# Three of five large projections by Strassen's algorithm, in a graph-attention and feed-forward kernel on one core

## The chip, the cores and the metric

The kernel runs on one core of one Trainium2 chip. A core has a matrix engine (TensorE, in the profile PE for its matmuls and PEld for its weight loads), VectorE (DVE), ScalarE (ACT), GpSimd (POOL) and SyncE (SP, here used to issue DMAs). The metric is the device time of one execution in microseconds, and of several runs the median. A profile is one execution, recorded by the hardware profiler.

## The reference, cut to what matters

Everything is fp32. `x` is 384 x 1024, all weights of the attention part are 1024 x 1024, the feed-forward part has a hidden width of 512.

```python
n = layernorm(x)
q, k, v = n @ wq.T + bq, n @ wk.T + bk, n @ wv.T + bv
q2, k2, v2 = q @ wiq.T + biq, k @ wik.T + bik, v @ wiv.T + biv      # then 16 heads of 64
scores = q2 @ k2.T / 8 + mask          # per head; mask from 12288 edges, -inf where there is none
x = x + (softmax(scores) @ v2) @ wo.T + bo
n = layernorm(x)
h = silu(n @ w1.T * s1) * (n @ w2.T * s2)
h = gelu(h @ h1.T * t1)
h = gelu(h @ h2.T * t2)
return x + h @ w3.T * s3
```

The mask is a 384 x 384 table: each edge (source, target, type) writes one value, the last edge of a cell wins, and the diagonal has a default.

## The kernel before, in words

Activations are held transposed (features on the 128 partitions, in 8 groups of 128, and the 384 rows in the free dimension), so that weights are TensorE's stationary operand and a projection needs no transposition. `matmul_T` (L139) makes one output group of 128 features: 8 matmuls of 128 x 128 weights with 384 columns, accumulated in one PSUM bank. `project` (L382) runs over two halves of the weights, each with four output groups; ScalarE writes each result to SBUF with the bias added (L391). The chain is qT from xT, q2T from qT, vT from xT, then v2 (rows on partitions, `matmul_R` at L148, 512 columns, evicted by VectorE at L404), then kT from xT. k2T is made in steps of one matmul (`project_k2`, L440): 24 steps ahead, the rest between the attention units.

Weights arrive in halves of 2 MB (`load_w`, L81) in a ring of four buffers; `prefetch` issues the next half on SP's queue. It waits until the half that it replaces has been read.

Beside the projections runs the making of the mask. Per chunk of 8 columns of 128 edges, `keys` (L325) reads the keys of the chunk back from memory, `targets` (L334) finds on VectorE the edges that a later edge overwrites, and `scatter` (L354) issues 8 indirect DMAs from POOL, each waiting for the one two before it. There are 12 chunks. In the program of VectorE all chunks stand ahead of the projections' own work, in SP's program the reads of the keys stand between the first weight loads. After the last scatter POOL reads the table back into `nmask` (L378), which every score reduction (L475) needs, and then adds the output bias to `xs` (L409).

The order on SP, ACT, DVE and PE is the order of the code (a manual schedule); each of these engines runs its instructions strictly one after the other, and waits on semaphores that the framework places. [...] two for the projections (`ps_mm`), the others for pools that open and close with the stages.

In the feed-forward part (`rest`, L616) ScalarE computes Silu at L687, and Gelu at L703 from h1 and h2. Before Gelu its table has to be loaded, which happens ahead of the first Gelu. `inspect` (L178) reads the feed-forward weights in pieces and sums the low halves of their words on ScalarE (L186), to choose between two ways of computing; the one used here has two fp32r products per weight.

Of the kernel before, what the change touches and what calls it, by code (L numbers as in the profile page):

```python
# [8 lines left out]
FP = mybir.dt.float32  # L9
FR = mybir.dt.float32r  # L10
BF = mybir.dt.bfloat16
# [4 lines left out]
ALU = mybir.AluOpType  # L16
# [11 lines left out]
NCOL = E // P  # L28
DEEP = 2
# [12 lines left out]
def gnn_ffn_kernel(ctx: ExitStack, tc: tile.TileContext, x, edges, etw, vecs, rows,  # L42
# [28 lines left out]
    row = const.tile([P, 3, F], FP, name="row")  # L71
# [5 lines left out]
    def load_rows():  # L77
        nc.sync.dma_start(row, bass.AP(tensor=rows.tensor, offset=rows.offset,
                                       ap=[[0, P], [F, 3], [1, F]]))
# [29 lines left out]
    biqs = const.tile([P, KF], FP, name="biqs")  # L109
# [68 lines left out]
    def inspect(raws):  # L178
        for raw in raws:
            at = lows.shape[1] - len(pieces)  # L180
            w, i = pieces.pop(0)
            nc.sync.dma_start(raw, bass.AP(tensor=w.tensor, offset=w.offset + i * P * F,
                                           ap=[[F, P], [1, F]]))
            low = raw.bitcast(U16).rearrange("p (f two) -> p f two", two=2)[:, :, 0]
            junk = stage.tile([P, F], BF, tag="junk", name="junk", bufs=1)
            nc.scalar.activation(junk, low, AF.Copy, accum_out=lows[:, at:at + 1])  # L186
# [3 lines left out]
    k2T = act.tile([P, KF, N], FP, name="k2T")  # L190
    v2 = act.tile([P, NT, F], FP, name="v2")
    xT = act.tile([P, KF, N], FP, tag="xT", name="xT")

    with tc.tile_pool(name="edge", bufs=1) as ep, tc.tile_pool(name="krow", bufs=2) as krp, \
# [20 lines left out]
        later = ep.tile([P, DEEP * P], FP, name="later")  # L215
# [149 lines left out]
        nc.vector.tensor_scalar(biqs, vec[:, BIQ:BIQ + KF], -0.125, None, op0=ALU.mult)  # L365
        for c0 in range(0, NCOL, CHUNK):
            kr = keys(c0)
            if c0 == 0:
                nc.sync.dma_start(cells, bare)
                prefetch()  # L370
            targets(c0, kr)
            if c0 == 0:
                values()
            scatter(c0)
            if c0 in (2 * CHUNK, 5 * CHUNK):
                prefetch()
        load_rows()
        read = nc.gpsimd.dma_start(nmask, cells).ins  # L378
        for i in sent[-DEEP:]:
            after(read, i)  # L380

        def project(src, name, bias, dst=None, scale=1.0):  # L382

            if dst is None:
                dst = act.tile([P, KF, N], FP, tag="t", name=name, bufs=2)
            for half in range(2):
                (w,) = queue.pop(0)
                for i in range(4):
                    o = 4 * half + i
                    ps = matmul_T(w, src, i)  # L390
                    nc.scalar.activation(dst[:, o, :], ps, AF.Identity, bias=bias[:, o:o + 1],  # L391
                                         scale=scale)
                prefetch()
            return dst

        qT = project(xT, "qT", vec[:, BQ:])
        project(qT, "q2T", biqs, dst=q2T, scale=-0.125)
        vT = project(xT, "vT", vec[:, BV:])
        for half in range(2):
            (w,) = queue.pop(0)  # L400
            c = slice(half * FH, (half + 1) * FH)
            for t in range(NT):
                ps = matmul_R(w, vT, t)
                nc.vector.tensor_add(v2[:, t, c], ps, row[:, 0, c])  # L404
            prefetch()

        for t in range(NT):
            tc.keep_in_program_order(
                nc.gpsimd.tensor_add(xs[:, t, :], xs[:, t, :], row[:, 1, :]))  # L409
        kT = project(xT, "kT", vec[:, BK:])  # L410
# [4 lines left out]
    aT = act.tile([P, KF, N], FP, tag="xT", name="aT")  # L415
    ps_ff = ctx.enter_context(tc.tile_pool(name="ps_ff", bufs=4, space=bass.MemoryType.PSUM))
# [17 lines left out]
    with tc.tile_pool(name="attn", bufs=1) as ap, \  # L434
# [5 lines left out]
        def project_k2():  # L440

            for o in range(KF):
                ps = ps_mm.tile([P, 512], FP, tag="mm", name="ps")
                for k in range(KF):
                    nc.tensor.matmul(ps[:, :N], lhsT=wik[o // 4][:, k, o % 4 * P:(o % 4 + 1) * P],  # L445
                                     rhs=kT[:, k, :], start=(k == 0), stop=(k == KF - 1))
                    if k == KF - 1:
                        nc.scalar.activation(k2T[:, o, :], ps[:, :N], AF.Identity,  # L448
                                             bias=vec[:, BIK + o:BIK + o + 1])
                        if o % 4 == 3:  # L450
                            early.append(load_w(*ffn[o // 4], rounded=True))
                    yield
# [163 lines left out]
    def rest(fast):  # L616
# [59 lines left out]
        for o in range(KH):  # L676
# [14 lines left out]
            if fast:  # L691
                nc.scalar.copy(g[0][:, o, :], full)
                remainder(g[1][:, o, :], full, g[0][:, o, :])

# [17 lines left out]
        for some in (ends[:3], *([e] for e in ends[3:])):  # L712
# [3 lines left out]
            for (t, a, b), (p, _) in zip(some, ps):  # L716
                nc.vector.tensor_mul(y[:, t, a:b], p, row[:, 2, a:b])  # L717
                nc.vector.tensor_add(y[:, t, a:b], y[:, t, a:b], xs[:, t, a:b])  # L718
                nc.sync.dma_start(out[t * P:(t + 1) * P, a:b], y[:, t, a:b])
# [39 lines left out]
```

## Time and profile before

| | us |
|---|---|
| median of 3 runs (414.23 to 414.82) | 414.78 |
| the profiled execution | 414.55 |
| its span in the trace | 412.8 |
| PE busy in the span | 402.2 |
| DVE busy | 151.4 |
| ACT busy | 114.7 |
| POOL busy | 109.9 |

A line of the list of groups reads: line of the kernel, engine, operation, output <- inputs (names without numbers), shapes, count, then busy time and the mean duration in ns of one, then the idle time of the engine just before them with what ended it. Durations of one engine can overlap: instructions are pipelined, so a mean duration is longer than the distance from one start to the next. In the chain of work that ended last, columns are the start, the length, and the engine and line that the chain went through. A line of the timeline has start, length, engine, line, operation, and in brackets the idle time before and what ended it. In the view of stretches each engine has its busy time and its number of instructions; then come the granted TensorE clock, the share of DMA, and GB/s. The 1.8 us between span and execution time are outside the trace.

### The profile page before, as it was taken

Reading aid. Unit: us, or ns where it says so; the run is one execution under the profiler, and the core shown is the slowest. Engines: PE = TensorE matmul, PEld = TensorE weight load, DVE = VectorE, ACT = ScalarE, POOL = GpSimd, SP = SyncE. Lnnn points to the kernel's source line nnn. Section 1 sums busy time; section 2 is a strip of 40 time slices with the busy share of each in tenths; the row PEclk is TensorE's granted clock in tenths of the full one; section 3 lists DMA queues with packets and bytes.
Section 4 is the critical chain, followed back from the end, with each engine's and each line's share of the span. In section 5 each row is a group of like instructions: output and inputs, shape, how many; then the busy total and the mean of one; then the engine's idle time right before and its main releaser. Section 6 shows DMA issues by size and latency. Waiting matters only on the chain.

```text
span 412.8 us, 4295 instructions
## 1 busy us (share of the span) xinstructions
PE 402.2 (97%) x1549; PEld 244.0 (59%) x1549; DVE 151.4 (37%) x525; ACT 114.7 (28%) x249; POOL 109.9 (27%) x117
## 2 busy tenths in 40 slices
PE   7899999999999999999999999999999999999993
PEld 7555555555555444455555555555554444699883
DVE  5637968600000001000000167866763045322455
ACT  4511111111111000001112156757672177132320
POOL 3023344332656465756474010000000000200000
PEclk9999999999999999999999999999999999999998
DMA  7699655997050505050517216111088040560004
GB/s 273 215 333 290 220 192 164 370 388 251 3 204 0 203 2 204 0 204 2 204 21 261 82 39 215 52 51 52 1 265 287 9 153 0 171 239 0 0 3 155
DMA packets 29208, 59.65 MB, mean 145 GB/s; under 512 B 4384, under 2 KB 7296, under 8 KB 29056
## 3 DMA queue, kind: packets, MB, share of 16 engines
q1 hardware_dynamic: 22016, 49.89, 35.1%
q0 software_dynamic: 6880, 9.03, 7.6%
q10 hardware_dynamic: 288, 0.41, 0.3%
q8 instruction: 14, 0.23, 0.2%
q14 instruction: 10, 0.08, 0.1%
HBM read 57.06 MB, written 2.26 MB: 144 GB/s over the span
## 4 chain that ended last, share of the span: by engine, by line
PE 90%; DVE 4%; ACT 3%; DMA 1%; issue 1%; SPq 0%; ACTq 0%
PE ps L144 40%; PE ps L153 10%; PE ps L445 10%; PE ps L424 8%; PE ps L625 6%; PE av L502 4%; PE sc L461 4%; PE pp L493 4%; PE ps L637 3%; DMA xs<-in_x 1%; DVE y L718 1%; DVE y L717 1%; DVE st L114 1%; ACT junk L186 1%; ACT e L477 1%
## 5 line engine op out<-in xcount | busy, mean ns | idle before, releaser
L356 POOL DMA_INDIRECT tab<-val,cell x96 | 94.4, 983 | 113.7 <-DMA tab<-val,cell 64.3
L475 DVE CUSTOM_DVE_ANT_0 e<-sc,nmask 128x384 f32<-128x384 f32 x48 | 23.9, 553 | 60.0 <-PE sc L461 59.9
L340 DVE SCALAR_TENSOR_TENSOR jk<-kr,key,later 128x256 bf16<-128x256 f32 x96 | 39.8, 479 | 13.9 <-DMA kr<-keyd 13.9
L445 PE MATMUL ps<-kT,wik 128*128 128x384 f32 x128 | 43.4, 487 | 0.0
L424 PE MATMUL ps<-wo,aT 128*128 128x512 f32 x96 | 42.5, 593 | 0.0
L144 PE MATMUL ps<-xT,wq 128*128 128x384 f32 x128 | 41.5, 487 | 0.3 <-ACT xT L260 0.3
L144 PE MATMUL ps<-qT,wiq 128*128 128x384 f32 x128 | 41.4, 486 | 0.0
L144 PE MATMUL ps<-xT,wv 128*128 128x384 f32 x128 | 41.4, 486 | 0.0
L144 PE MATMUL ps<-xT,wk 128*128 128x384 f32 x128 | 41.4, 486 | 0.0
L153 PE MATMUL ps<-wiv,vT 128*128 128x512 f32 x96 | 41.4, 592 | 0.0
L404 DVE TENSOR_TENSOR v<-ps,row 128x512 f32<-128x512 f32 x6 | 4.1, 691 | 95.9 <-PE ps L153 95.9
L144 PEld LDWEIGHTS ps<-xT,wk 128*128 128x128 f32 x128 | 24.3, 190 | 17.2 <-issue 0.5
L144 PEld LDWEIGHTS ps<-xT,wq 128*128 128x128 f32 x128 | 24.2, 190 | 17.2 <-ACT xT L260 0.5
L144 PEld LDWEIGHTS ps<-qT,wiq 128*128 128x128 f32 x128 | 24.3, 190 | 17.0
L144 PEld LDWEIGHTS ps<-xT,wv 128*128 128x128 f32 x128 | 24.3, 190 | 17.0
L477 ACT ACTIVATE e<-e,lo 128x384 f32<-128x384 f32 x48 | 28.9, 604 | 12.0 <-DVE lo L475 11.4
L445 PEld LDWEIGHTS ps<-kT,wik 128*128 128x128 f32 x128 | 23.5, 190 | 14.6 <-ACT k2T L448 0.5
L153 PEld LDWEIGHTS ps<-wiv,vT 128*128 128x128 f32 x96 | 18.2, 190 | 22.7 <-issue 22.5
L424 PEld LDWEIGHTS ps<-wo,aT 128*128 128x128 f32 x96 | 17.7, 190 | 20.2 <-issue 20.2
L391 ACT ACTIVATE kT<-ps,vec 128x384 f32<-128x384 f32 x8 | 4.6, 581 | 77.8 <-PE ps L144 77.8
L625 PE MATMUL ps<-x,w 128*128 128x384 f32 (+2 forms) x176 | 25.8, 307 | 0.0
L625 PEld LDWEIGHTS ps<-x,w 128*128 128x128 f32 x176 | 25.1, 190 | 0.5 <-issue 0.5
(112 smaller groups left out, 367.6 us busy)
## 6 DMA issues: line engine op xcount, KB each, us to landing
kr<-keyd SPq DMA_DIRECT2D x11, 576.0 KB, 5.6
raw<-in_w SPq DMA_DIRECT2D x12, 512.0 KB, 4.8
w<-in_w POOLq DMA_DIRECT2D x3, 2048.0 KB, 11.0
wiq<-in_wiq SPq DMA_DIRECT2D x2, 2048.0 KB, 14.0
wv<-in_wv SPq DMA_DIRECT2D x2, 2048.0 KB, 15.4
wiv<-in_wiv SPq DMA_DIRECT2D x2, 2048.0 KB, 14.6
wk<-in_wk SPq DMA_DIRECT2D x2, 2048.0 KB, 8.3
wik<-in_wik SPq DMA_DIRECT2D x2, 2048.0 KB, 7.6
```

The costliest lines, as they stand in the source:

```text
L144: nc.tensor.matmul(ps[:, :N], lhsT=w[:, k, o * P:(o + 1) * P], rhs=src[:, k, :], start=(k == 0), stop=(k == nk - 1))
L153: nc.tensor.matmul(ps[:, :w.shape[2]], lhsT=src[:, k, t * P:(t + 1) * P], rhs=w[:, k, :], start=(k == 0), stop=(k == nk - 1))
L340: nc.vector.scalar_tensor_tensor(jk[:, :w], krf[:, j * P:j * P + w], key[:, c:c + 1], later[:, :w], op0=ALU.is_equal, op1=ALU.mult, accum_ ...
L356: i = nc.gpsimd.indirect_dma_start(out=tab, in_=val[:, c:c + 1], in_offset=None, out_offset=bass.IndirectOffsetOnAxis(ap=cell[:, c:c + 1], ...
L424: nc.tensor.matmul(ps, lhsT=aT[:, k, t * P:(t + 1) * P], rhs=wos[half][:, k, :], start=k == 0, stop=k == KF - 1)
L445: nc.tensor.matmul(ps[:, :N], lhsT=wik[o // 4][:, k, o % 4 * P:(o % 4 + 1) * P], rhs=kT[:, k, :], start=(k == 0), stop=(k == KF - 1))
L461: nc.tensor.matmul(sc[:, :N], lhsT=q2T[r, pair, t * P:(t + 1) * P], rhs=k2T[r, pair, :], start=True, stop=True)
L475: nc.vector.tensor_tensor_reduce(e, sc[:, :N], nmask[:, t, :], 1.0, 3e38, op0=ALU.add, op1=ALU.min, accum_out=lo)
L477: nc.scalar.activation(e, e, AF.Exp, bias=lo, scale=-1.0, accum_out=dens[u][:, j:j + 1])
L493: nc.tensor.transpose(pt[:, m, :], e[:, m * P:(m + 1) * P], ident)
L502: nc.tensor.matmul(av[j * D:(j + 1) * D, :N], lhsT=v2[:, m, h * D:(h + 1) * D], rhs=pTs[pair % 2][:, j * NT + m, :], start=(m == 0), stop= ...
L625: nc.tensor.matmul(ps[:, rows], lhsT=w[:, k, o * P:(o + 1) * P], rhs=x[:, k, rows], start=n == 0, stop=n == len(todo) - 1)
```

## The change

The projections q2, v and k are computed by Winograd's form of Strassen's algorithm, one level deep. Features in (two halves of 4 groups), features out (two weight halves) and rows (two halves of 192) are halved. Seven products of 4 x 4 matmuls with 192 columns take the place of eight such (64 matmuls of 384 columns before). The weight sums are made in place in the weight buffers and in one extra buffer `t3`; the sums of the source are four blocks `sums`, made once from xT (used by v and k) and once from qT. Results are put together by VectorE from PSUM and from what is already in the output; ScalarE copies only the first product. q and v2 keep their form; v2 and k2T take their inputs in the order 4 to 7, 0 to 3.

Other edits: the chunks of the mask are no longer all ahead, but one by one between the steps of the projections, on VectorE and SP; weight loads are issued in pairs after q2, v and k; `ps_st` has 6 banks; the factor -0.125 moves from q2T to k2T; the three constant rows take two places, and the third row is loaded later; `later` lies in `jp`; the sums of the low halves are written in place instead of into `junk`; k2T and v2 share memory with the sums; and an activation of one column with Gelu is put behind the Silu stage.

```diff
-            junk = stage.tile([P, F], BF, tag="junk", name="junk", bufs=1)
-            nc.scalar.activation(junk, low, AF.Copy, accum_out=lows[:, at:at + 1])
+            nc.scalar.activation(low, low, AF.Copy, accum_out=lows[:, at:at + 1])
...
-        for c0 in range(0, NCOL, CHUNK):
-            kr = keys(c0)
-            if c0 == 0:
-                nc.sync.dma_start(cells, bare)
-                prefetch()
-            targets(c0, kr)
-            if c0 == 0:
-                values()
-            scatter(c0)
-            if c0 in (2 * CHUNK, 5 * CHUNK):
-                prefetch()
-        load_rows()
+        krs = [keys(0)]
+        nc.sync.dma_start(cells, bare)
+        def chunk():
+            c0 = len(sent)
+            if c0 + CHUNK < NCOL:
+                krs.append(keys(c0 + CHUNK))
+            targets(c0, krs.pop(0))
+            if c0 == 0:
+                values()
+            scatter(c0)
...
+        def row_sums(src, tag):
+            sums = act.tile([P, 4, HK, HN], FP, tag=tag, name="sums")
+            s1, s2, s3, s4 = (sums[:, i] for i in range(4))
+            (a11, a12), (a21, a22) = ([src[:, k:k + HK, r:r + HN] for k in (0, HK)]
+                                      for r in (0, HN))
+            minus(s3, a11, a21)
+            nc.vector.tensor_add(s1, a21, a22)
+            minus(s2, s1, a11)
+            minus(s4, a12, s2)
+            return s1, s2, s3, s4
+        def third(at=0):
+            b11, b12, b21, b22 = blocks(at)
+            t3 = tp.tile([P, HK, FH], FP, tag="t3", name="t3")
+            minus(t3, b22, b12)
+            return t3
+        def first():
+            b11, b12, b21, b22 = blocks()
+            minus(b12, b12, b11)
+        def product(w, x):
+            ps = [ps_st.tile([P, 2, 256], FP, tag="st", name="ps") for _ in range(2)]
+            for o in range(4):
+                for k in range(HK):
+                    nc.tensor.matmul(ps[o // 2][:, o % 2, :HN], lhsT=w[:, k, o * P:(o + 1) * P],
+                                     rhs=x[:, k, :], start=(o % 2, k) == (0, 0),
+                                     stop=(o % 2, k) == (1, HK - 1))
+            return [p[:, :, :HN] for p in ps]
...
+            def plus(to, ps, more):
+                for p in range(2):
+                    o = slice(2 * p, 2 * p + 2)
+                    nc.vector.tensor_add(to[:, o, :], ps[p], more[:, o, :])
+            def finish(to, ps, more, column):
+                for o in range(4):
+                    nc.vector.scalar_tensor_tensor(
+                        to[:, o, :], ps[o // 2][:, o % 2, :], bias[:, column + o:column + o + 1],
+                        more[:, o, :], op0=ALU.add, op1=ALU.add)
+            m1 = product(b11, a11)
+            for p in range(2):
+                nc.scalar.copy(c11[:, 2 * p:2 * p + 2, :], m1[p])
+            beside[0]()
+            m7 = product(t3, s3)
+            nc.vector.tensor_add(b11, b11, t3)
+            beside[1]()
+            m6 = product(b11, s2)
+            plus(c12, m6, c11)
+            plus(c21, m7, c12)
+            m2 = product(b21, a12)
+            beside[2]()
+            finish(c11, m2, c11, 0)
+            minus(b21, b21, b11)
+            m5 = product(b12, s1)
+            plus(c12, m5, c12)
+            finish(c22, m5, c21, HK)
+            beside[3]()
+            finish(c12, product(b22, s4), c12, HK)
+            finish(c21, product(b21, a22), c21, 0)
+            for _ in range(2):
+                queue.pop(0)
+                prefetch()
...
-        qT = project(xT, "qT", vec[:, BQ:])
-        project(qT, "q2T", biqs, dst=q2T, scale=-0.125)
-        vT = project(xT, "vT", vec[:, BV:])
+            prefetch()
+            chunk()
+            prefetch()
+            chunk()
+            prefetch()
+            sums_x = row_sums(xT, "k2T")
+            chunk()
+            load_rows(0, 0, 2)
+            qT = project(xT, "qT", vec[:, BQ:])
+            t3 = third()
+            first()
+            chunk()
+            sums_q = row_sums(qT, "v2")
+            t3s = []
+            project_fast(qT, sums_q, t3, q2T, vec[:, BIQ:],
+                         [nothing, chunk, chunk, lambda: t3s.append(third(2))])
+            vT = act.tile([P, KF, N], FP, tag="t", name="vT", bufs=2)
+            project_fast(xT, sums_x, t3s[0], vT, vec[:, BV:], [first, chunk, chunk, chunk])
+            v2 = act.tile([P, NT, F], FP, tag="v2", name="v2")
             for half in range(2):
...
+                prefetch()
+                for _ in range(2 - half):
+                    chunk()
+                if half == 0:
+                    t3 = third(1)
...
-        kT = project(xT, "kT", vec[:, BK:])
+            kT = act.tile([P, KF, N], FP, tag="t", name="kT", bufs=2)
+            project_fast(xT, sums_x, t3, kT, vec[:, BK:], [first, nothing, nothing, nothing])
...
+        loaded = small.tile([P, 1], FP, name="loaded")
+        nc.scalar.activation(loaded, eps, AF.Gelu)
```

`blocks` names the four blocks of two weight halves: left half's upper and lower inputs are b11 and b21, the right half's are b12 and b22. Products are numbered here in the order in which they run: m1, m7, m6, m2, m5, and the two last ones. `chunk` in the list `beside` puts one chunk of the mask's work at that point.

## The prediction

> **What bounds the kernel now.** First the page's busy times and the chain that ended last:
>
> ```profile
> span 412.8 us, 4295 instructions
> PE 402.2 (97%) x1549; PEld 244.0 (59%) x1549; DVE 151.4 (37%) x525; ACT 114.7 (28%) x249; POOL 109.9 (27%) x117
> PE 90%; DVE 4%; ACT 3%; DMA 1%; issue 1%; SPq 0%; ACTq 0%
> ...
> PE ps L144 40%; PE ps L153 10%; PE ps L445 10%; PE ps L424 8%; PE ps L625 6%; PE av L502 4%; PE sc L461 4%; PE pp L493 4%; PE ps L637 3%; DMA xs<-in_x 1%; DVE y L718 1%; DVE y L717 1%; DVE st L114 1%; ACT junk L186 1%; ACT e L477 1%
> ```
>
> TensorE is the chain: L144, the four projections q, q2, v and k, is 40% of the span alone. The change touches three of them. Next the chain in order of time, for lengths without overlap, and the groups kept apart by shape:
>
> ```profile
> 12.96 124.08 PE ps L144 x384
> 137.04 41.20 PE ps L153 x96
> 178.24 41.28 PE ps L144 x128
> ```
>
> ```profile
> L144 PE MATMUL ps<-qT,wiq 128*128 128x384 f32 x128 | 41.4, 486 | 0.0
> L144 PEld LDWEIGHTS ps<-qT,wiq 128*128 128x128 f32 x128 | 24.3, 190 | 17.0
> L718 DVE TENSOR_TENSOR y<-y,xs 128x512 f32<-128x512 f32 x5 | 3.5, 693 | 0.2
> L718 DVE TENSOR_TENSOR y<-y,xs 128x256 f32<-128x256 f32 x2 | 0.8, 425 | 0.1
> L531 DVE COPY pTa<-pp 128x384 f32<-128x384 f32 x12 | 6.7, 557 | 9.9 <-PE pp L493 9.9
> L689 DVE SCALAR_TENSOR_TENSOR gf<-ps,vec,sl 128x384 f32<-128x384 f32 x4 | 2.5, 618 | 14.5 <-PE ps L625 14.5
> ```
>
> A projection of 64 fp32 matmuls leaves 128 records. Records of 384 columns follow each other at 41.28/128 = 322.5 ns, those of 512 columns at 41.20/96 = 429.2 ns: 0.833 ns a column and 2.5 ns for the record. (The 486 of the page is a duration with drain; it overlaps.) PE has no idle time here, and its weight loads are idle 17 of 41 us: they hide. Other engines in those 206 us, by the view of stretches (columns: PE, PEld, DVE, ACT, POOL busy):
>
> ```profile
> 13.00:54.00 41.00, 41.00 (x128) 24.17 (x129) 26.68 (x125) 7.35 (x12) 10.53 (x10) 1.00 0.83 270
> 54.00:95.00 41.00, 41.00 (x129) 24.17 (x128) 21.74 (x108) 4.66 (x8) 15.99 (x16) 1.00 0.77 269
> 95.00:137.00 42.00, 42.00 (x132) 24.77 (x131) 0.00 (x0) 4.66 (x8) 24.36 (x26) 1.00 0.30 101
> ```
>
> DVE is empty from 95 us on; that is the room the change uses.
>
> [...] 32 of the 128x256 records of L625 take 3.83 us of the chain, 120 ns each, each with its load. [...] In this trace a scatter instruction takes 1.0 to 1.2 us beside DVE work and 0.97 later, so little. [...]
>
> **The change part by part.**
>
> *PE.* Each of q2, v, k becomes seven products of 4 x 4 matmuls of 192 columns: 112 matmuls, 224 records instead of 128. At 192 x 0.833 + 2.5 = 162.5 ns these take 36.4 us. The old ones took 41.36 (124.08/3), 41.36 and 41.28. Saved: 4.96 + 4.96 + 4.88 = 14.8 us, if the records stay at that pitch. No 192-column fp32 record is in the trace. Below: 160 ns is pure streaming, 35.8 us. Above: the only records [...] are the fp32r ones of 384 columns at L625; 59 of them touch 10 us of trace, some 172 ns each, giving 38.5 us and a saving of only 8.5 us in all. I take 162.5: the 2.5 ns is the same at 384 and 512 columns of fp32[...].
>
> *DVE.* Per projection four sums of 2048 elements (t3, b12, b11, b21) at 2.29 us = 9.2; six adds from PSUM of 384 elements at 0.56 (the L531 duration) = 3.3; twelve finishes of 192, estimated as L689's 618 less 192 elements at 1.05 = 0.42 us, = 5.0: 17.5 us. Row sums of xT and qT: eight of 768 at 0.96 = 7.7. Together 60 us, on top of 52.6 busy in that stretch, in some 191 us. So DVE is not the bound by volume; order decides. With E the start of a projection, products of 5.2 us, and an edge chunk of 3.7 us (18.18 to 21.92 us in the timeline):
> Product 3 needs b11+t3, which waits for product 1 to have read b11: E+5.4+2.3 = 7.7, against 10.4. In k DVE comes from the last chunk and `first()`, and is done near E+9.0: 1.4 to spare, the tightest.
> Product 5 needs the banks of product 2, freed by the four adds after product 3: E+15.8+2.2 = 18, against 20.8.
> Product 7 needs b21-b11: after a chunk and finishes, E+25.6, against 31.2.
> The v2 matmuls need vT's finish of product 6, behind v's third chunk: E+33.9, against 36.4; they begin with the late inputs' half that is ready first, and the last finish hides behind four matmuls.
> All on time, so the sums cost nothing while DVE keeps this order; a DVE that is 3 us late in a projection starts to stall PE.
>
> *SP.* The key reads are now issued between weight loads. In v, the keys of its second chunk stand behind wiv0 and wiv1, which wait for q2's last product. The DMA row reaches 370 and 388 GB/s in 72 to 93 us; 4.2 MB and 0.6 MB of keys at that pace with 2 us of latency land near E+15; the chunk comes at E+18. In q2 the keys behind wv1 land near 65 us, the chunk can begin as late as 68. Nothing on the path.
>
> *POOL.* The scatters and the mask:
>
> ```profile
> 211.20 0.97 POOL L356 DMA_INDIRECT tab<-val,cell  x1 [0.30 <-issue]
> 213.96 0.80 POOL L378 DMA_DIRECT2D nmask<-tab  x1 [1.79 <-DMA tab<-val,cell]
> ```
>
> The read takes 4.3 us to land, at 218.3; the first score row needs it at 235.88, and after the change at 221.1. A scatter costs 1.28 us undisturbed (most of 103 to 117 us), nearer 2.5 under loads (16 in 54 to 95). After: some 15 by 66 us as before, 19 more by 91 (no weight load then, chunks 4 to 6 ready), and 62 at 1.6 (the 26 in 42 of the stretches): last at about 191, mask near 198. The last chunk is ready near 173, not binding.
>
> *ACT.* The Gelu load:
>
> ```profile
> 386.95 1.28 ACT L703 ACT_TABLE_LOAD   x1 [2.27 <-PE ps L637]
> 388.25 1.05 ACT L703 ACTIVATE gf<-ps,vec 128x384 f32<-128x384 f32 x2
> ```
>
> ```profile
> 383.24 5.71 PE L637 MATMUL ps<-g,h 128*128 128x384 f32 x32
> 389.28 0.45 PE L637 MATMUL ps<-g,h 128*128 128x384 f32 x1 [0.32 <-DVE g L705]
> 389.87 5.67 PE L637 MATMUL ps<-g,h 128*128 128x384 f32 x31
> ```
>
> The dummy goes behind the last copy of the gate (ends 384.7), so the load ends at 386.0 in ACT's idle time. ACT gains 1.28, but PE works on the fourth output until about 388.8 (388.95 less drain), then loses 0.5 ahead of 389.28 and 0.4 ahead of 389.87. That 0.9 is the gain; then PE is what is late. The in-place copy of the raw pieces (1.06 us each) keeps its elements: taken as nothing, bounded by 0.5 us either way, as ACT waits anyhow in those stages. Bias and scale moved to k2T: same instruction count.
>
> Sum: 414.55 of the profiled run - 14.8 - 0.9 = 398.9; the median (414.78) stands 0.2 above that run: 399.1 us. Attention moves up whole.
>
> **The rivals.**
> (1) PE stalls at seams: DVE late by waiting for keys or by slower sums. For: DVE is strict in order, and a chunk that waits for keys holds finishes that free banks. Against: the margins above. Each stall is 1 to 3 us in one or two projections: 400.5 to 405.
> (2) Records of 192 columns keep 172 ns: 414.8 - 8.5 - 0.9 = 405.4, with small waits 405 to 408. For: the fp32r records. Against: fp32 records show no such gap.
> (3) The mask comes late. If POOL contends with the 2.3 us sums and chunks wait, the scatters end after 215 and the first scores wait at L475 while PE goes on only with the k2T steps left. It costs from a mask at 221.1 on, and decides for slower at 221.1 + 15.7 = 236.8, when the last scatter is at 231: a mean of (231-24.65)/96 = 2.15 us a scatter, against 1.95 before (a few us more if k2T steps fill in). At the 2.5 of the loaded stretch throughout, the last is at 265 and the mask lands near 271, 50 us late, of which k2T steps in PE's order fill perhaps 5: 399 + 45 = 444, an estimate. Against: the loads end sooner, and POOL has 30 us of slack by my count.
> (4) The dummy is useless, if Gelu's load stays where it was: 400.0. The program of the change has a load ahead of the dummy and none ahead of Gelu, so unlikely; it is inside the first range.
>
> **How the numbers follow.** Forecast (398 to 400.5) 0.62; stalls (400.5 to 405) 0.18; record gap (405 to 408) 0.12; better than 398, from a cause I don't see, 0.03; mask late 0.05, of which 0.04 ends slower and 0.01 level. The range takes forecast and stalls: 397.8 to 405. Three runs before lie within 0.6 us, so 0.2%, 0.8 us, is about what can be told from no change. Faster 0.95, same 0.01, slower 0.04.
>
> **What would show it.** Right: 672 records of 192 columns in three stretches of 36.4 us with no PE idle; Gelu without a table load ahead and PE gapless near 374; the mask's read issued well before 221; DVE busy for about 113 us between 13 and 205. Wrong: stretches of 38.5 us without idle (gap of the record); PE waiting for DVE sums or finishes (rival 1), with DVE waiting for kr; the first score reduction waiting for the mask's DMA (rival 3).

## The result, and the profile after

The changed kernel takes 409.23 us (median of 4 runs, 408.51 to 411.07), the kernel before 414.77 beside it (4 runs, 414.23 to 414.82): 0.988 of the time, with an interval of 0.984 to 0.991. That is 5.5 us faster, and 10.1 us slower than the 399.1 predicted. (Runs more than 1.5% above the fastest of their kernel are left out of the ratios; medians and ranges hold all runs.)

The busy times and the chain that ended last, from the page of the changed kernel:

```profile
span 406.5 us, 4951 instructions
PE 389.9 (96%) x1837; PEld 281.3 (69%) x1837; DVE 211.4 (52%) x611; ACT 106.3 (26%) x232; POOL 123.3 (30%) x117
PE 69%; DMA 11%; POOL 8%; issue 4%; DVE 4%; ACT 3%; SPq 0%; POOLq 0%; ACTq 0%
```

Before, the chain was 90% PE, now 69%. The scatters of `tab`, the table of the mask, are 16% of it (10% their landings, 6% their instructions): for 77 us, from 149 to 226 us, the end of the kernel hangs on them and no longer on TensorE. The projections themselves, from the same chain in order of time (start, length):

```profile
13.03 41.52 PE ps L146 x128
54.55 72.80 PE ps L430 x448
127.35 20.61 PE ps L508 x48
```

L430 is the product of the seven. q2 and v together are 448 records in 72.80 us: 36.4 each, 162.5 ns a record, where before three projections took 41.28 to 41.36 each. VectorE's part of it, and that of POOL, in the stretch of q2's products (columns as in the prediction):

```profile
54.00:92.00 38.00, 38.00 (x234) 37.80 (x233) 25.59 (x65) 1.54 (x3) 21.38 (x18) 1.00 0.42 149
```

PE is busy throughout. The weight loads now fill nearly all of the stretch too (37.80 of 38.00), and still nothing waits for them.

The time is lost at the mask. From the timeline, POOL's last scatter and the read of the mask, and VectorE's first score reduction:

```profile
223.76 0.97 POOL L355 DMA_INDIRECT tab<-val,cell  x1 [0.30 <-issue]
226.51 0.80 POOL L517 DMA_DIRECT2D nmask<-tab  x1 [1.79 <-DMA tab<-val,cell]
231.09 0.56 DVE L591 CUSTOM_DVE_ANT_0 e<-sc,nmask 128x384 f32<-128x384 f32 x1 [25.36 <-DMA nmask<-tab]
```

Before, the last scatter was issued at 211.20 and the read at 213.96. So the scatters, which the forecast had ending at 191, end 12.6 us later than before. The reduction was due at 221.3 (that is where it stands below, where the mask is early); it waits until 231.09. Those 9.8 us are the miss: 408.51 of the profiled run less 9.8 is 398.7, against 398.9 forecast for it.

TensorE's view of the same moment, from its timeline:

```profile
225.92 0.92 PE L577 MATMUL sc<-k2T,q2T 64*128 64x384 f32 x4
231.70 2.12 PE L577 MATMUL sc<-k2T,q2T 64*128 64x384 f32 x4 [4.87 <-DVE lo L591]
234.62 1.51 PE L609 MATMUL pp<-ident,e 128*128 128x128 f32 x6 [0.79 <-POOL xs L523]
235.92 3.94 PE L561 MATMUL ps<-kT,wik 128*128 128x384 f32 x8
```

PE's own idle time is 4.87 + 0.79 us. Most of the rest is the clock, which the view of stretches shows ahead of the share of DMA:

```profile
225.00:230.00 5.00, 1.83 (x8) 0.54 (x6) 0.00 (x0) 0.00 (x0) 3.47 (x3) 1.00 0.40 105
230.00:235.00 5.00, 2.50 (x6) 1.39 (x7) 2.94 (x8) 1.31 (x4) 4.29 (x2) 0.65 0.04 15
235.00:240.00 5.00, 5.00 (x16) 3.05 (x16) 4.07 (x15) 4.62 (x12) 0.95 (x1) 0.67 0.05 13
```

The granted clock was 0.50 from 231.5 to 238.3 us, and 1.00 before and after. The four score records take 2.12 us instead of the 0.92 of those at 225.92, the six records of L609 1.51 instead of the 0.88 of six at 241.28, and the eight k2T records of the last row 3.94 instead of 8 x 0.3225 = 2.58, together 3.2 us; with the idle time that is 8.9 of the 9.8 us. The clock fell 4.7 us after the end of the last matmul (226.84), and the first k2T records after it lie 640 ns apart instead of 322.5.

The groups of POOL's scatters, before and after:

```profile
L356 POOL DMA_INDIRECT tab<-val,cell x96 | 94.4, 983 | 113.7 <-DMA tab<-val,cell 64.3
```

```profile
L355 POOL DMA_INDIRECT tab<-val,cell x96 | 108.0, 1125 | 112.7 <-DMA tab<-val,cell 66.2
```

The same 96 instructions, the same idle time between them, of which 64.3 and 66.2 us are waits for the scatter two before to land; but 13.6 us more busy. The timelines of POOL and VectorE say where:

```profile
76.65 3.09 POOL L355 DMA_INDIRECT tab<-val,cell  x1 [0.30 <-issue]
82.59 2.90 POOL L355 DMA_INDIRECT tab<-val,cell  x1 [0.30 <-issue]
```

```profile
76.61 2.28 DVE L394 TENSOR_TENSOR wiq<-wiq 128x2048 f32<-128x2048 f32 x1
82.36 2.28 DVE L394 TENSOR_TENSOR t<-wv 128x2048 f32<-128x2048 f32 x1
```

A scatter that begins while one of the new weight sums runs ends 0.84 us after that sum: here the sums end at 78.89 and 84.64. Nine scatters begin so (a tenth in the last 10 ns of a sum), all with these 0.84 us; one that begins 0.4 us ahead of a sum still takes its 0.97 us (at 115.59 and at 160.70). Before, no scatter was longer than 1.2 us. Added up over all 96, what is above 0.97 us was 1.4 us and is 14.9, of which 13.0 belong to the nine that a sum holds.

The Gelu table, in ACT's timeline:

```profile
379.54 1.28 ACT L811 ACT_TABLE_LOAD   x1
381.82 1.06 ACT L821 ACTIVATE gf<-ps,vec 128x384 f32<-128x384 f32 x2 [0.78 <-PE ps L753]
```

The load now ends before the first Gelu has its input, and PE's two gaps behind L637 are gone: its records of L753 follow each other without a gap from 378.10 on.

### The profile page after: what moved, and what is told of

It reads as the page before. It is cut to its first block, busy times and chain, and to the rows that moved or that the text cites. A ratio compares the mean times of both kernels' runs of the same rounds, so it can differ in the third digit from the quotient of the medians.

```text
span 406.5 us, 4951 instructions
## 1 busy us (share of the span) xinstructions
PE 389.9 (96%) x1837; PEld 281.3 (69%) x1837; DVE 211.4 (52%) x611; ACT 106.3 (26%) x232; POOL 123.3 (30%) x117
## 4 chain that ended last, share of the span: by engine, by line
PE 69%; DMA 11%; POOL 8%; issue 4%; DVE 4%; ACT 3%; SPq 0%; POOLq 0%; ACTq 0%
PE ps L430 18%; PE ps L146 10%; DMA tab<-val,cell 10%; PE ps L540 8%; POOL tab L355 6%; PE ps L741 6%; PE ps L508 5%; PE ps L561 5%; PE pp L609 4%; PE av L618 4%; PE ps L753 4%; PE sc L577 4%; POOL xs L523 2%; ACT raw L187 1%; DMA xs<-in_x 1%
## 5 line engine op out<-in xcount | busy, mean ns | idle before, releaser
L355 POOL DMA_INDIRECT tab<-val,cell x96 | 108.0, 1125 | 112.7 <-DMA tab<-val,cell 66.2
L339 DVE SCALAR_TENSOR_TENSOR jk<-kr,key,jp 128x256 bf16<-128x256 f32 x96 | 39.8, 478 | 15.0 <-DMA kr<-keyd 15.0
L561 PE MATMUL ps<-kT,wik 128*128 128x384 f32 x128 | 44.6, 497 | 0.0
L561 PEld LDWEIGHTS ps<-kT,wik 128*128 128x128 f32 x128 | 24.1, 196 | 14.9 <-issue 1.1
L609 PEld LDWEIGHTS pp<-ident,e 128*128 128x128 f32 x144 | 16.7, 144 | 13.0 <-issue 5.6
L577 PE MATMUL sc<-k2T,q2T 64*128 64x384 f32 x96 | 20.5, 529 | 4.9 <-DVE lo L591 4.9
L609 PE MATMUL pp<-ident,e 128*128 128x128 f32 x144 | 21.2, 284 | 0.8 <-POOL xs L523 0.8
L95 POOL DMA_DIRECT2D w<-in_w x3 | 2.6, 861 | 61.9 <-PE ps L561 60.0
L187 ACT ACTIVATE raw<-raw 128x1024 uint16<-128x1024 uint16 x16 | 21.1, 1342 | 0.0
L601 DVE TENSOR_SCALAR e<-e,rd 128x384 f32<-128x384 f32 x48 | 19.0, 438 | 0.9
L95 POOL DMA_DIRECT2D h<-in_h x2 | 1.5, 759 | 53.1 <-issue 53.1
```

The source lines that it names most:

```text
L187: nc.scalar.activation(low, low, AF.Copy, accum_out=lows[:, at:at + 1])
L339: nc.vector.scalar_tensor_tensor(jk[:, :w], krf[:, j * P:j * P + w], key[:, c:c + 1], later[:, :w], op0=ALU.is_equal, op1=ALU.mult, accum_ ...
L355: i = nc.gpsimd.indirect_dma_start(out=tab, in_=val[:, c:c + 1], in_offset=None, out_offset=bass.IndirectOffsetOnAxis(ap=cell[:, c:c + 1], ...
L577: nc.tensor.matmul(sc[:, :N], lhsT=q2T[r, pair, t * P:(t + 1) * P], rhs=k2T[r, pair, :], start=True, stop=True)
L609: nc.tensor.transpose(pt[:, m, :], e[:, m * P:(m + 1) * P], ident)
```

## The experiments

The theory (A): the sum of the change is right, and what is missing is the lateness of the mask, which comes from scatters held up by the long sums of VectorE. Rivals: (B) the weight loads, which now come in pairs, delay the landings of the scatters; (C) something in the seven products themselves costs the time, and the mask is only seen waiting. All times in one table. The groups of kernels ran on different chips, by number in the last column (for the first two rows it is not on record). The kernel before ran beside each group: 414.52 us on chip 7, 414.78 on 13, 414.42 on 6 and 414.51 on 1.

| kernel | median us | range, runs | chip |
|---|---|---|---|
| before, beside the first of these | 414.77 | 414.23 to 414.82, 4 | - |
| changed | 409.23 | 408.51 to 411.07, 4 | - |
| without the mask's read | 408.36 | 404.41 to 410.58, 4 | 7 |
| without the weight sums | 408.81 | 406.4 to 411.55, 4 | 7 |
| wo's loads behind the mask | 413.56 | 406.02 to 416.59, 17 | 7 |
| weight sums in four pieces | 407.07 | 403.11 to 411.35, 4 | 7 |
| half of the scatters | 399.75 | 399.43 to 399.8, 4 | 13 |
| k plain, wo behind the mask | 404.92 | 404.4 to 405.51, 4 | 13 |
| four scatters in flight | 399.93 | 399.8 to 400.85, 4 | 13 |
| before, with the dummy Gelu | 413.84 | 413.28 to 414.09, 12 | 13 |
| before, four scatters in flight | 431.84 | 420.61 to 449.4, 4 | 6 |
| the same, scatters spaced | 421.03 | 419.82 to 422.12, 4 | 1 |
| without the weight sums, spaced | 416.14 | 415.28 to 417.85, 6 | 1 |

### Without the read of the mask

```diff
-            read = nc.gpsimd.dma_start(nmask, cells).ins
-            for i in sent[-DEEP:]:
-                after(read, i)
```

The attention then works on what `nmask` held before: the edges have no effect.

> The changed kernel without the read of the table into nmask: the scores get the initial diagonal pattern in place of the edges' mask, so the mask part of the computation is left out; scatters, sums and products stay. Theory (the late mask is the whole of the missing gain): the first score reduction runs near 221.3 us in place of 231.1, no 25 us wait for the mask, and the time falls by 9.8 us to about 399 (398 to 400.5). Rival (DVE's sums or the slower in-place copy on ACT cost part of it elsewhere): the time falls by clearly less, to 402 or more.

Measured 408.36, ratio 0.982 (0.974 to 0.990). The edit missed its aim, as the waits of this kernel show:

```profile
DVE e L588 <- DMA tab<-val,cell: 20.3, 1, 20.3
```

The first reduction still waited, now for the last scatter itself: its output `e` takes over the memory of `val` and `cell`, the scatters' inputs. It began at 226.11, 5 us earlier than with the read, 4.8 later than due. So the read is not what has to be earlier; the end of the scatters is. The range of 6 us from run to run comes back below.

### Half of the scatters

```diff
-            for c in range(c0, c0 + CHUNK):
+            for c in range(c0, c0 + CHUNK // 2):
```

Half of the edges are left out; chunks, sums, loads and products stay.

> The changed kernel with only the first four of each chunk's eight scatters (half of the edges are left out of the mask; sums, products, loads and the mask's read stay). In the two runs that had the mask in time, PE lost time in steps of 0.7 us in the k products, without a releaser in the trace, while scatters ran at full pace beside it. Theory (what is missing from the forecast is the scatters' alone: their end, and what their full pace does to the 192-column products): no wait for the mask, no such steps, and the forecast's own sum, 399 (398 to 400.5). Rival (the steps, or DVE's sums, belong to the new projections whatever POOL does): 403 or more, with steps of 0.7 us in the k products.

Measured 399.75, ratio 0.9636 (0.962 to 0.965). The mask's read, and what the first reductions wait for:

```profile
182.58 0.80 POOL L517 DMA_DIRECT2D nmask<-tab  x1 [1.80 <-DMA tab<-val,cell]
```

```profile
DVE e L591 <- PE sc L577: 18.6, 3, 15.6
```

With a mask that is early, reductions wait for scores alone, the first begins at 221.31, and the kernel takes what the forecast's sum gave: 399.75 against 399.1. All that the prediction said of PE, DVE, SP and ACT holds to 0.7 us together, and C falls in its plain form.

### Without the weight sums, and with them in four pieces

```diff
-            minus(t3, b22, b12)
-            return t3
+            return b22
...
-            minus(b12, b12, b11)
...
-            nc.vector.tensor_add(b11, b11, t3)
...
-            minus(b21, b21, b11)
```

The products then use blocks of the weights instead of their sums, so the output is not the projection's.

> The changed kernel without the twelve 2048-element sums of weight blocks (t3 is b22 itself, b12, b11 and b21 stay as loaded), so the three projections are wrong in value; everything else stays. Theory A (POOL is held while a long DVE sum with two SBUF inputs runs): the mean scatter instruction falls from 1125 to about 985 ns, 13 us in all, the mask's read is issued near 214 in place of 226.5, and the time falls to 399 to 401. Rival B (the weight and key transfers hold the scatters, the sums do not): scatter instructions get shorter by less than 3 us in all, the read stays at 222 or later, the time at 405 or above.

The group of the scatters, and TensorE's timeline in k:

```profile
L355 POOL DMA_INDIRECT tab<-val,cell x96 | 94.7, 987 | 110.2 <-DMA tab<-val,cell 57.6 <-issue 20.9 <-DVE val L322 20.6
```

```profile
197.19 0.65 PE L428 MATMUL ps<-sums,wk 128*128 128x192 f32 x3 [0.28 <-issue]
198.59 1.05 PE L428 MATMUL ps<-sums,wk 128*128 128x192 f32 x4 [0.75 <-issue]
200.02 1.06 PE L428 MATMUL ps<-sums,wk 128*128 128x192 f32 x5 [0.38 <-issue]
...
205.02 0.42 PE L428 MATMUL ps<-xT,wk 128*128 128x192 f32 x1 [0.40 <-issue]
207.13 1.12 PE L428 MATMUL ps<-xT,wk 128*128 128x192 f32 x3 [1.69 <-issue]
```

As A expects, a scatter is back at 987 ns without the sums (983 before), and the mask is on time (read at 210.84). Yet the kernel took 408.81, ratio 0.984 (0.979 to 0.989): 10 us more than A said. In the trace, which is of a run of 411.55, the products of k go in steps of 1.4 us with PE idle in between, for no releaser that the profile knows ("issue"), and k2T begins at 217.23 instead of 204.79. Something else had taken the place of the late mask.

```diff
-            minus(t3, b22, b12)
+            for k in range(HK):
+                minus(t3[:, k, :], b22[:, k, :], b12[:, k, :])
```

(and the other three sums alike: four of 512 elements each.)

> The changed kernel with each 2048-element weight sum cut into four of 512. If POOL is held only until the running DVE instruction ends, a scatter that meets a sum waits at most 0.6 us in place of up to 2.2, scatter instructions shrink by about 8 of the 14 extra us, the read is issued near 219 and the time is about 402. If the back-to-back sums hold POOL as one, the scatter mean stays near 1125 ns and the time at 409. DVE's own work grows by about 12 x 0.2 us, which has room.

407.07, ratio 0.977 (0.972 to 0.982), with the scatters at

```profile
L355 POOL DMA_INDIRECT tab<-val,cell x96 | 98.6, 1027 | 120.0 <-DMA tab<-val,cell 68.2 <-issue 22.5 <-DVE val L322 20.8
```

Shorter sums hold a scatter for less (1027 ns in the mean, against 1125 with whole sums and 987 without), so here it is the length of one sum that counts, not the volume. But the mask was hardly earlier (read at 224.45): landing waits grew to 68.2 us. These waits are more than half of POOL's idle time, and much larger than the 13.6 us of the sums.

### What makes the landings late

In k the two halves of wo are loaded while the last scatters go out, and POOL waited 3.38, 0.95, 4.65 and 2.44 us for landings between 204 and 218. Rival B says that these loads do it.

```diff
+                load = queue.dma_start(...)
+                if name.startswith("wo"):
+                    held(load.ins)        # held = lambda load: after(load, read)
```

> The changed kernel with the two wo loads made to wait on SP's queue until the mask has been read back. Theory: the waits of the last scatters behind wo0 and wo1 (3.4, 0.9, 4.7 and 2.4 us after 200.8) go, about 10 us; the read is issued near 216, the mask lands near 220.5, and the time falls to 399 to 401. wo is needed only near 300. Rival (what is taken away comes back, since the scatters wait as long for other transfers or for the table's own writes): the read stays later than 222 and the time above 405.

The group of the scatters and the mask's read:

```profile
L359 POOL DMA_INDIRECT tab<-val,cell x96 | 106.5, 1110 | 105.1 <-DMA tab<-val,cell 50.8 <-issue 23.8 <-DVE val L326 20.8
217.49 0.80 POOL L521 DMA_DIRECT2D nmask<-tab  x1 [1.79 <-DMA tab<-val,cell]
```

B holds for its part: landing waits fall from 66.2 to 50.8 us (to 58.9 in the next kernel, which holds these loads too, so by 7 to 15 us), the mask is 9 us earlier and nothing waits for it. And again the gain was lost in k: 413.56 in the median of 17 runs, and a ratio of 0.985 (0.981 to 0.988) from the three that it leaves in. The trace is of a run of 415.11, in which PE waits on "issue" 14 times in k for 8.0 us, in the same steps, and the first scores come at 236.0; what the three runs did in k is not known. So two kernels in which the scatters follow each other more freely lost their gain in the products of k.

```diff
-            project_fast(xT, sums_x, t3, kT, vec[:, BK:], [first, nothing, nothing, nothing])
+            kT = project(xT, "kT", vec[:, BK:])
```

(k as before the change, wo behind the mask, q2 and v by seven products.)

> The kernel with the wo loads held behind the mask, and k computed plainly again (64 matmuls of 384 columns); q2 and v by seven products. The first scores are due near 226, the mask lands near 220. Theory (the 0.7 us steps need 192-column records, with a weight load under every 162 ns, beside full-paced scatters): no steps, 399 + 4.9 = 404 (403 to 405.5). Rival (they come with any PE work when no large load interrupts the scatters): steps in the plain k as well, 408 or more.

404.92, ratio 0.9758 (0.974 to 0.977). No steps, mask's read at 217.91, every score reduction waits for scores alone. That is 5.2 us over the kernel with half of the scatters, where a projection left plain should cost 4.9; nothing else is lost, and the rest of the change is worth what it was said to be. That the steps need the records of 192 columns is not shown by it: this kernel ran on another chip than the two with steps (see the end of this part).

### Four scatters in flight

```diff
-DEEP = 2
+DEEP = 4
...
-        bare = ep.tile([P, NT, N], FP, name="bare")
+        bare = act.tile([P, NT, F], FP, tag="v2", name="bare")[:, :, :N]
```

A scatter then waits for the one four before it; for this VectorE compares against 512 later edges instead of 256, and the keys of a chunk are 11 columns instead of 9. (The second edit makes room.)

> The changed kernel with four scatters in flight in place of two (DEEP = 4): each key is compared with 512 later ones in place of 256, so a chunk takes DVE 5.7 us in place of 3.7. Theory (the last scatter is late because each waits for the landing of the one two before): those waits, 66 us, mostly go; the last scatter is paced by the last chunk and issued near 190, the mask lands near 197, no wait for it. DVE is then late at v's third chunk by about 4 us: about 403 (400 to 405). Rival (the waits return at the deeper depth since the transfers are held for as long): the mask's read later than 215 and 408 or more.

399.93, ratio 0.9649 (0.963 to 0.966): faster than both kernels, by 14.8 and 9.3 us. The group, the mask's read and the projections:

```profile
L355 POOL DMA_INDIRECT tab<-val,cell x96 | 112.8, 1175 | 72.8 <-issue 24.7 <-DVE val L322 23.0 <-DMA tab<-val,cell 15.5
```

```profile
191.70 0.81 POOL L517 DMA_DIRECT2D nmask<-tab  x1 [1.79 <-DMA tab<-val,cell]
```

```profile
54.57 72.80 PE ps L430 x448
168.57 36.63 PE ps L430 x224
```

The scatter instructions are longer than ever (1175 ns instead of 1125, beside comparisons of 747 ns instead of 478; the one at 169.34 takes 1.46 us), but the landing waits fall from 66.2 to 15.5 us, and the mask is 35 us earlier. VectorE's longer comparisons (235.9 us busy instead of 211.4) did not make it late, against what was expected: k took 36.63 instead of 36.4, and that is all. The kernel is bound by TensorE again: its chain is 90% PE.

### The dummy Gelu alone

```diff
+        loaded = small.tile([P, 1], FP, name="loaded")
+        nc.scalar.activation(loaded, eps, AF.Gelu)
```

> The kernel before with the dummy Gelu alone. Forecast: PE's two gaps before h2 close, 0.9 us: ratio 0.9978 (0.9970 to 0.9985). Rival (the load costs nothing in the kernel before, because PE works on the fourth output meanwhile): ratio 1.000.

413.84 against 414.78: ratio 0.9973 (0.9964 to 0.9982), 0.8 to 1.5 us at the ends of the interval and 0.9 between the medians. The forecast had 0.9, worked out from two gaps of PE; both are gone in the trace.

### The steps in k: when TensorE's signals come late

A control: is it the mask alone that four scatters in flight help? In the kernel before, the mask was early anyway.

> The kernel before with four scatters in flight instead of two (and `bare` in the memory of `v2`), a control for the version with four scatters: is the time that they bring the mask's alone? In the kernel before the mask landed at 218.3 and was needed at 235.9, so an earlier mask is worth nothing there. Theory (four scatters in flight help the changed kernel only because its mask is late): 414.8, within 0.8 of before, with the mask's read issued 15 to 25 us earlier than 213.96. Rival (overlapped scatters also take something from the weight loads, the DVE or the products, or give something to them): more than 1 us away from 414.8.

The time is 420.61 to 449.4 in four runs. By its number the rival holds, and 2.0 us are a wait of PE for the weights wv, which it names; the rest neither theory had. The trace is of the run of 427.42. TensorE's timeline in v2, and VectorE's evictions of it:

```profile
139.22 20.98 PE L153 MATMUL ps<-wiv,vT 128*128 128x512 f32 x48
162.95 10.16 PE L153 MATMUL ps<-wiv,vT 128*128 128x512 f32 x16 [2.76 <-DVE v L404]
```

```profile
152.31 0.69 DVE L404 TENSOR_TENSOR v<-ps,row 128x512 f32<-128x512 f32 x1 [57.64 <-remote]
162.20 0.69 DVE L404 TENSOR_TENSOR v<-ps,row 128x512 f32<-128x512 f32 x1 [9.20 <-remote]
174.90 1.29 DVE L404 TENSOR_TENSOR v<-ps,row 128x512 f32<-128x512 f32 x2 [12.01 <-remote]
```

PE begins v2 at 139.22, and 16 records of 429.2 ns later, at 146.1, its first bank is complete. VectorE, which has been idle since 94.7, begins to read it at 152.31; the second, complete at 153, at 162.20. PE then waits for its banks. In the kernel before, the same evictions begin within 0.1 us of the bank's end (143.94 after 143.91). "remote" means that the profile found no instruction whose end fits the signal. The trace also records each update of a semaphore, and there the signal is: 20 ns ahead of each of these evictions stands the update of TensorE's semaphore, at 152.29, 162.18 and 174.88. It is not VectorE that hesitates, it is TensorE's update that comes 6 us, then 9, then 15 us after the matmuls that raise it.

With these updates paired in order to the matmuls that raise them, the kernels fall into two sorts. No update comes over 1 us late in the kernel before, with half of the scatters, with k plain, with the dummy Gelu and with four in flight in the changed kernel; the runs of each of these lie within 1.3 us. In the kernel without weight sums updates come 2 to 5 us late from 187 us on, 14 at 197, and the steps begin there; with wo held, 2 at 189 and up to 17 at 200, the same; with the sums in pieces up to 5. (Without the read, five records are missing just there, and nothing can be said.) The ranges of these runs are 5 to 11 us. The changed kernel itself has 3.5 us once, at 112, and 2.3 at 189, behind which no PE time is lost. In these six traces, the control's among them, 1 to 5 records of such updates are missing, in all the others none. Two of the control's missing ones belong to banks that ScalarE nevertheless took on time, at 113.62 and 118.78, so there the record is missing and not the signal. A suspect is the pace of the scatters, 1.28 us from start to start: 17 and 18 in a row (125 to 170 us) in the control, and three times 8 with little between (177 to 208) in the kernel without weight sums. Two more kernels have the scatters spaced:

```diff
             for c in range(c0, c0 + CHUNK):
+                nc.gpsimd.memset(nmask[:, 0, :], 0.0)
                 i = nc.gpsimd.indirect_dma_start(
```

> The kernel before with four scatters in flight, and ahead of each scatter a memset of 128 x 384 on GpSimd (about 0.4 us, from 1.06 us for 1152 columns at L203), so that scatters follow at 1.7 us or more instead of 1.28. With four in flight and no memsets, runs of 17 and 18 scatters without a gap (112 to 170 us) went together with TensorE's semaphore updates coming up to 15 us after the matmuls that raise them. Theory (the pace of the scatters alone delays those updates): no update over 1 us late, 414 to 416, the mask's read near 200 to 215. Rival (four in flight, or v2's place in memory, delays them, whatever the pace): 420 or more, with the vector engine again waiting at L404 or elsewhere for updates that come late.

> The changed kernel without the weight sums of 2048 elements (the output is then not the product of the weights: t3 is b22 itself, b11, b12 and b21 stay as loaded), as before, and with the same memset of 128 x 384 on GpSimd ahead of each scatter. Without the memsets this kernel took 408.8: the mask was on time, but TensorE's updates came up to 14 us late in k from 186 us on and its products then went in steps of 0.7 us. Theory (the pace of the scatters does both): no late updates, no steps, k's products in 36.4 us; the mask's read at 212 to 222, thus 399 to 404. Rival (something else in the combination of two scatters in flight and 192-column products): steps again, 407 or more.

In both no update comes over 1 us late. With four in flight in the kernel before, VectorE's evictions of v2 are back to one every 6.87 us, each with its bank:

```profile
148.95 0.69 DVE L405 TENSOR_TENSOR v<-ps,row 128x512 f32<-128x512 f32 x1 [53.25 <-PE ps L153]
155.82 0.69 DVE L405 TENSOR_TENSOR v<-ps,row 128x512 f32<-128x512 f32 x1 [6.17 <-PE ps L153]
```

and k's products of the other kernel follow each other without steps:

```profile
189.00 10.56 PE L429 MATMUL ps<-sums,wk 128*128 128x192 f32 x64
199.40 5.36 PE L429 MATMUL ps<-xT,wk 128*128 128x192 f32 x32
```

The times are no gain, for other reasons: 421.03, since there wv comes late (PE waits 2.94 us for it and then takes 43.09 us for v's 128 records instead of 41.44, at a granted clock of 0.96 in the mean: 4.6 us together), and 416.14, since the memsets and the landings together push the mask's read to 233.22, later than the 222 expected. The memsets are not spread evenly, either: in places three run ahead and scatters follow at 1.28 us behind them, so "spaced" is a lower density over tens of us, not a fixed distance.

What makes the updates late stays open. That it is the scatters is not shown, for two reasons. First, density doesn't sort the kernels: the one with k plain has 23 scatters in its densest 30 us, between 185 and 215, as many as the control and the two kernels with steps, and no late update; the one with the sums in pieces has 21, like the kernel before, and updates up to 5 us late. Second, the chip does sort them: all four kernels of chip 7 and the one of chip 6 have late or missing updates, none of the six of chips 13 and 1 has (the chip of the changed kernel, with its few, is not on record). The spaced kernels ran on another chip than the kernels that they are compared with, so thinning the scatters and changing the chip can't be told apart; only the kernel before ran on all four, within 0.4 us. Nor can it be said how much belongs to the recording of the trace, since every measured run was recorded, and records are missing in just those traces that have late ones.

## Why the prediction was wrong

By its own steps:

*PE* was right: 672 records of 192 columns at 162.5 ns, with no PE idle, 36.4 us each in q2, v and k. The rival of a longer pitch (172 ns) is out; that L625's records are a measure for it was not shown. Nor was it that the weight loads fit under such records; this run shows it, with loads busy 37.80 of 38.00 us in q2 and nothing waiting for them.

*DVE* was right in its conclusion: sums of 2.28 to 2.29 us, and row sums of 0.95 to 0.96, all on time, also where they share the engine with longer comparisons. (An estimate from the prediction's lines of 512 and 256 elements, 693 and 425 ns, gives by their slope 2.30 us at 2048 and 0.96 at 768.) The prediction counted twelve finishes per projection; there are sixteen, at 0.41 us. DVE was busy for 111.3 us between 13 and 205, against 113.

*SP* was right in its conclusion for the keys: VectorE waits for none in v, 3.28 us in q2 (until 65.36) and 5.12 in v2 (until 157.44), with PE busy throughout. (Where it has 2 us of latency, the trace before has 1.6 us from issue to landing for 48 KB of `keyd`, and 2.2 for a scatter.) It left out the other side of the paired loads, wo's during the last scatters: 7 to 15 us of landing waits.

*ACT* was right: 0.9 us for the table, measured alone as 0.9. The in-place copy was not free of cost but of consequence: 1342 ns instead of 1057, 16 times, off the path.

*POOL* is the step that failed, and it is a sum of a count, a pace and a duration. It put 34 scatters by 91 us, then 62 at 1.6 us, the last at about 191. The trace has 26 by 91 (25 before), and 70 at 1.90 to 223.76. The count and the pace failed in part because most of the landing waits were taken to vanish with the loads; they stayed, 64.3 before, 66.2 after. The duration failed at one sentence. The prediction priced what VectorE costs a scatter by the kernel before, 1.0 to 1.2 us in place of 0.97, as "so little". But no sum of 2048 elements was in the kernel before; no VectorE instruction that the scatters met there was longer than 0.69 us. The change adds twelve of 2.28 us, and a scatter that begins beside one takes up to 3.09 us in place of 0.97. All scatters together are 13.6 us longer, against 12.6 by which they end later than before. Without these sums the mask's read was issued at 210.84 instead of 226.51. A plain estimate from the prediction's own 2.29 us was at hand: twelve sums, each taken to hold one scatter for its own length, are 27 us.

The slack was mis-stated too. "30 us of slack by my count" rested on the forecast of 191. Against what the trace showed, the mask landing at 218.3 and the new need at 221.1, it was 2.8 us. Any cost to POOL above that was on the path, and the estimate of 27 us was ten times as much.

*The rivals.* The third came true, at a chance of 0.05: mask late, by POOL's contention with the sums, from 221.1 on. The point from which it costs was right; its far side (slower from a mask at 236.8) was not reached, as the mask came at 231.09. (For that side the last scatter would be at 229.7 and not 231, since the mask lands 7.1 us after it in the kernel before.) Its chance was given to slower and level alone; a late mask that leaves the kernel 5.5 us faster, which is what came, had none. The first (stalls at seams) did not occur in the changed kernel. The fourth is out.

The sum without the POOL step stands: 399.75 with half the scatters, 399.93 with four in flight, against 399.1.

## What to carry to other kernels

When a change brings the end of one chain forward, take the slack of every other chain from its measured end in the trace, not from a forecast of how that will improve as well: here 2.8 us, not 30. Where the change adds longer instructions beside another engine's work, price that work by the longest of them and not by what it met before (here 3.09 us a scatter beside a sum of 2.28, 1.2 beside what was there before), and see whether a wait that is independent of it (here two scatters in flight, 66 us of landing waits) can be taken away to give the slack back; four in flight turned a gain of 5.5 us into 14.8. Try such a remedy in the kernel that needs it: in the kernel before, the same edit cost 6 us or more.

Run two kernels that are to be compared on the same chip. Here the kernel before took the same time on four chips, and yet the late updates of other kernels can't be put down to an edit, because each edit ran on one chip alone.

## What the runs showed of the hardware that was not expected

- In the changed kernel, the nine scatter instructions on POOL that begin while one of VectorE's fp32 sums of 2048 elements runs end 0.84 us after that sum: up to 3.09 us beside sums of 2.28, against 0.97 alone, and 0.97 where one began 0.4 us ahead of the sum. With the sums cut to 512 elements the mean of all scatters is 1027 ns instead of 1125, without them 987. Why a sum holds a scatter was not shown.
- TensorE's semaphore updates came late in some kernels: up to 15 us after the matmul in the control, with VectorE idle in that time, and 14 to 17 us in two kernels in which PE went in steps of 1.4 us. Seen on two of four chips, while scatters went out densely; the cause is open, and chip, scatters and the recording are not told apart.
- The 192-column fp32 records follow each other at 162.5 ns, on the line through those of 384 and 512 columns (322.5 and 429.2 ns), with the weight loads busy 37.80 of 38.00 us.
- ScalarE's pass over every second uint16 of 2048, written in place, took 1342 ns; written to bf16 elsewhere, 1057 (16 of each).
